# Shorter warm-up products, and the look-ups of largest weights moved forward, in a transformer layer in float32

## The chip, the cores and the metric

The kernel runs on one core of one Trainium2 chip. The metric is the device time in microseconds (us) of one execution. TensorE multiplies, VectorE (DVE in the profile), ScalarE (ACT) and GpSimd (POOL) do the elementwise work, and SyncE (SP) issues most of the transfers.

## The reference

Four sequences of 2048 tokens with 256 features go through one layer: an attention over chunks of 32 tokens with a gate, a layer norm, a gated feed-forward part whose weights are integers, and a second layer norm.

```python
Q = x @ W_q.T; K = x @ W_k.T; V = x @ W_v.T
decay = sigmoid(log_decay[0])                       # one scalar
mask = where(diff >= 0, decay ** diff, 0)           # 32 x 32
S = einsum('bncd,bnkd->bnck', Qc, Kc) * mask        # inside chunks of 32
O = einsum('bnck,bnkd->bncd', S, Vc)
attn = sigmoid(x @ W_g.T) * O @ W_o.T + x
x = layernorm(x + attn)
wg, wu, wd = w_gate / 127, w_up / 127, w_down / 127 # int32, drawn from -127 to 127
h = silu(x @ wg.T) * (x @ wu.T)                     # 768 hidden features
x = layernorm(x + h @ wd.T)
```

## The kernel before

The 8192 tokens are worked on in 16 blocks of 512 (`TB`). Everything is unrolled, and most instructions are kept in the order of the program on their engine (`in_turn`), so the order of the calls below is the order of each engine's queue. All intermediate data stay on the chip.

**Precision.** Most float32 products are made of three cheaper ones: a factor is split into a high and a low part and a "gap" term (`weight_parts`, `token_parts`), `three` multiplies high by high and low by low, lets ScalarE scale the bank (L527), and adds the product of the gaps afterwards (`rest()`, `g_rest()`, `others()`). The products have names by what they make: p_g (gate), p_v (values), p_y (scores' left factor), p_o (output projection). The first block is multiplied without splitting (pg, pv, py, pa), since its split weights aren't there yet.

**The feed-forward weights** come as nine integer pieces of 128x512: three each of `fg_int`, `fu_int` and `fd_int`, in this order numbered 0 to 8. ScalarE casts each piece to a high (fp32r) and a low (f16) copy. The split is exact only for integers up to a bound; so for each piece VectorE also looks up the largest magnitude in each row (`look_up`, L293, one TENSOR_REDUCE per piece into a column of `top`). Then `count_wide` compares `top` with the bound (`wide`, L305), adds up over the rows with a product by ones (`pw`, L309), reduces that to one number (`count`, L311) and copies it as an integer (`n_wide_early`, L1164). At the end of the program the engines read that number, and a slow path runs only if it isn't zero.

**The head.** At the start the transfers of the first weights and tokens are issued, SP taking xT and ScalarE's queue taking wg in halves. While they are under way TensorE multiplies zeros with zeros, with the column counts of `WARM` (L193, bank `pi`); these products end before pg, the gate of block 0 (L572). A float32 product is run in two passes over its columns. Then follow pv, pm (the product of two weight matrices), py, the split products of block 1, the scores and values of block 0 (ps, po), goT and pa. The sequence around the moved look-ups is:

```python
v_1, rest = split_v(1, x_parts)
cast_fg(0)
look_up([0])
sT = attn_scores(0, yT)
xTs[2] = load_xT(2)
g_rest()
rest()
look_up([1, 2])
yT, rest = split_y(1, x_parts)
goT = attn_values(0, sT, v, sg, by_half=True)
```

Some 15 us later block 0's normalized h is transposed on TensorE (`transpose_h`, bank `pt`), ScalarE makes hT_hi of it and VectorE hT_lo; `look_up([3])` stands behind that in VectorE's queue, and `gate()`, the two tanh of p_g into sg, on ScalarE. After that the output product's gap terms and the first chunk of the feed-forward part (fg, fu) follow.

**The loop** over blocks `b` interleaves block b's feed-forward chunks `hc` 0 to 5 (`ffn_up`: products fg and fu, silu on ScalarE giving s, VectorE's u = fu * s, ScalarE's u_hi, GpSimd's u_lo) with the attention of blocks b+2 and b+3. In its first pass, `look_up(range(4, 6))` stands between goT and chunk 4's u, and the last three look-ups behind chunk 5's u; in its second pass the count stands behind chunk 5.

**Banks.** The eight PSUM banks are given out from one pool in turn (`bank`). A new product's bank is one whose earlier content must have been read.

Of the kernel before, what the change touches and what calls it, by code (L numbers as in the profile page):

```python
# [47 lines left out]
F32 = mybir.dt.float32  # L48
F32R = mybir.dt.float32r
F16 = mybir.dt.float16  # L50
I32 = mybir.dt.int32
AF = mybir.ActivationFunctionType
ALU = mybir.AluOpType
# [9 lines left out]
EXACT = 128.0  # L63
# [6 lines left out]
SHIFT = 2.0**12  # L70
TOP = 1.0 - 0.5 / SHIFT
WHOLE = 1.0 + 1.0 / SHIFT
WARM = 512, 512, 128


@with_exitstack
def kernel(
# [15 lines left out]
    nc = tc.nc  # L93
# [7 lines left out]
    const = ctx.enter_context(tc.tile_pool(name="const", bufs=1))  # L101
# [12 lines left out]
    def in_turn(ins):  # L114
        tc.keep_in_program_order(ins)

    def bank(name):
        return psum.tile([P, TB], F32, tag="ps", name=name)
# [17 lines left out]
    def load_xn(b, start=None):  # L136
        xn = xin.tile([P, NG, D], F32, tag="x", name=f"x_{b}")
        src = x[span(b, start), :].rearrange("(g p) d -> p g d", p=P)
        queue(start).dma_start(xn, src)
        return xn  # L140
# [50 lines left out]
    pi = bank("pi")  # L191
    for n in WARM:
        nc.tensor.matmul(  # L193
            pi[:, :n],
            lhsT=nc.const_aps.tensor(0.0, [P, P]),
            rhs=nc.const_aps.tensor(0.0, [P, n]),
            start=True,
            stop=True,
# [88 lines left out]
    n_pieces = sum(map(len, ffn_int))  # L287
    top = const.tile([P, n_pieces], F32, tag="top", name="top")

    def look_up(which):  # L290
        pieces = [piece for pieces in ffn_int for piece in pieces]
        for i in which:
            reduced = nc.vector.tensor_reduce(  # L293
                top[:, i : i + 1],
                pieces[i].rearrange("p k n -> p (k n)"),
                mybir.AxisListType.X,
                ALU.max,
                apply_absolute_value=True,
            )
            tc.keep_in_program_order(reduced)  # L300

    def count_wide():

        wide = const.tile([P, top.shape[1]], F32, tag="wide", name="wide")
        nc.vector.tensor_scalar(wide, top, EXACT, None, ALU.is_gt)  # L305
        ones = const.tile([P, 1], F32, tag="ones", name="ones")
        nc.vector.memset(ones, 1.0)
        pw = bank("pw")
        nc.tensor.matmul(pw[:1, : top.shape[1]], lhsT=ones, rhs=wide, start=True, stop=True)  # L309
        count = const.tile([1, 1], F32, tag="count", name="count")  # L310
        nc.vector.tensor_reduce(count, pw[:1, : top.shape[1]], mybir.AxisListType.X, ALU.add)  # L311
        return count

    def free(ins):
        pass
# [101 lines left out]
    def normalize(r, scale, shift, groups=range(NG)):  # L417
        for g in groups:
            in_turn(
                nc.scalar.activation(  # L420
                    r[:, g, :],
                    r[:, g, :],
                    AF.Identity,
                    bias=shift[:, g : g + 1],
                    scale=scale[:, g : g + 1],
                )
            )
# [120 lines left out]
    def split_y(b, x_parts):  # L548
        yT = work.tile([P, KD, TB], F32, tag="yT", name=f"yT_{b}")

        def finish(i, pb):
            in_steady_turn(nc.vector.tensor_copy(yT[:, i, :], pb))

        return yT, three(f"y_{b}", feature_major(w_parts["m"], x_parts), finish)
# [479 lines left out]
    xTs[2] = load_xT(2)  # L1034
    g_rest()
    rest()
    look_up([1, 2])
    yT, rest = split_y(1, x_parts)
    goT = attn_values(0, sT, v, sg, by_half=True)
    cast_fg(1)  # L1040
# [21 lines left out]
    sg, g_rest = split_gate(2, x_parts)  # L1062
    normalize(hs[0], *scales_h)
    y_rest()
    gate = g_rest(hold=True)
    hs[1], out_rest = split_out(1, go_parts)
    hTs[0] = transpose_h(0, hs[0])
    look_up([3])
    gate()
    x_parts, x_gaps = token_parts(xTs[3], "x_3")  # L1070

# [21 lines left out]
    for b in range(NB - 2):  # L1093
        n = b + 2
        m = b + 3
        more = m < NB
        xns[n] = load_xn(n)
        if b and m + 1 < NB:
            xTs[m + 1] = load_xT(m + 1)
        hT = hTs.pop(b)  # L1100
        uT = ([], []) if b else uT_0
        sT, v, sg = ahead
        if not more:
            scales_next = iterated_scale_and_shift(mv_out, of_out, f"out_{b}")
        if b:
            normalize(hs[b + 1], *scales_h)
            up_now(b, hT, uT, 0)
        multiply = ffn_up(b, hT, uT, range(1, 2), held=True)
        if b:
            moving = move_h(b + 1, hs[b + 1])  # L1110
        else:
            cast_fd(0, range(2, 3))
            multiply()
            x_gaps()
            sT = attn_scores(n, yT)
            xTs[m + 1] = load_xT(m + 1)
        if more:
            yT, y_rest = split_y(m, x_parts)
        if b:
            multiply()  # L1120
        if not more:
            goT = attn_values(n, sT, v, sg)
        multiply = ffn_up(b, hT, uT, range(2, 3), held=True)
        if b > 1:
            normalize(r_before, *scales_out, range(NG // 2))
        multiply()
        if more:
            y_rest()
        if b == 0:
            normalize(hs[b + 1], *scales_h)  # L1130
            moving = move_h(b + 1, hs[b + 1])
        if not more:
            go_parts, go_gaps = token_parts(goT, f"go_{n}")
        multiply = ffn_up(b, hT, uT, range(3, 4), held=True)
        if b > 1:
            normalize(r_before, *scales_out, range(NG // 2, NG))
        multiply()
        if b > 1:
            store(b - 2, r_before)
        if more:  # L1140
            sT_next = attn_scores(m, yT)
            goT = attn_values(n, sT, v, sg)
            if b == 0:
                look_up(range(4, 6))
            multiply = ffn_up(b, hT, uT, range(4, 5), held=True, low_first=True)
            go_parts, go_gaps = token_parts(goT, f"go_{n}")
            if b == 0:
                cast_fd(1, range(1))
            multiply()
            go_gaps()  # L1150
            v_next, v_rest = split_v(m, x_parts)
            sg_next, g_rest = split_gate(m, x_parts)
            v_rest()
            if b == 0:
                cast_fd(1, range(1, 2))
            up_with_cast(b, hT, uT, 5, 1, range(2, 3))
            if b == 0:
                look_up(range(6, n_pieces))
            if b == 1:
                count = count_wide()  # L1160
                n_wide_early = const.tile(
                    [1, 1], I32, tag="n_wide_early", name="n_wide_early"
                )
                nc.vector.tensor_copy(n_wide_early, count)  # L1164
        else:
            up_now(b, hT, uT, 4)
            go_gaps()
        r_before = r_out
        if more:
            hs[n], out_rest = split_out(n, go_parts)  # L1170
            if b:
                hTs[b + 1] = split_h(b + 1, moving)
            g_rest()
            mv_h = out_rest()
            if b == 0:
                hTs[b + 1] = split_h(b + 1, moving)
            ahead = sT_next, v_next, sg_next
            if m + 1 < NB:
                x_parts, x_gaps = token_parts(xTs[m + 1], f"x_{m + 1}")
            std_h = root_in_turn(mv_h, of_h, f"h_{b}")  # L1180
            if b:
                mv_before, std_before = mv_out, root_in_turn(mv_out, of_out, f"out_{b}")
            back_to_silu()

            def between():
                scales = scale_and_shift(
                    mv_h, std_h, of_h, f"h_{b}", nc.vector, in_turn
                )
                if m + 1 < NB:
                    x_gaps()  # L1190
                return scales

            r_out, mv_out, scales_h = ffn_down(b, uT, hs.pop(b), between)
            if b:
                scales_out = scale_and_shift(mv_before, std_before, of_out, f"out_{b}")
        else:
            multiply = ffn_up(b, hT, uT, range(5, KH), held=True)
            hs[n], out_rest = split_out(n, go_parts)
            multiply()
            hTs[b + 1] = split_h(b + 1, moving)  # L1200
            scales_out = scales_next
            normalize(r_before, *scales_out)
            store(b - 1, r_before)

            def amid():
                return iterated_scale_and_shift(out_rest(), (HALF, 1.0), f"h_{n}")

            r_out, mv_out, scales_h = ffn_down(
                b, uT, hs.pop(b), chunkwise=True, amid=amid
            )  # L1210
            scales_out = iterated_scale_and_shift(mv_out, of_out, f"out_{b + 1}")
# [361 lines left out]
```

## Time and profile before

| | |
|---|---|
| time, median of 3 runs | 490.38 us (490.08 to 491.08) |
| the profiled execution's own time | 490.36 us |
| its span, from first to last instruction | 488.6 us |
| TensorE busy | 482.2 us (99% of the span) |
| VectorE, ScalarE, GpSimd busy | 338.1, 374.7, 281.2 us |
| look-ups (L293), each | 0.67 to 0.69 us, first at 21.3 us, last at 70.1 us |
| pw (L309) | at 97.1 us |
| warm-up products (L193) | 1.00 to 5.18 us |

In the profile PE is TensorE's products, PEld its weight loads, which overlap them; an engine's name with a q is its queue. A row of a timeline gives the start, the duration, the engine, the line, the operation, what it writes and reads, and in brackets how long the engine was idle before and what ended that. "x4" is the number of instructions in the row.

### The profile page before, as it was taken

Reading aid. Unit: us, or ns where it says so; the run is one execution under the profiler, and the core shown is the slowest. Engines: PE = TensorE matmul, PEld = TensorE weight load, DVE = VectorE, ACT = ScalarE, POOL = GpSimd, SP = SyncE. Lnnn points to the kernel's source line nnn. Section 1 sums busy time; section 2 is a strip of 40 time slices with the busy share of each in tenths; the row PEclk is TensorE's granted clock in tenths of the full one; section 3 lists DMA queues with packets and bytes.
Section 4 is the critical chain, followed back from the end, with each engine's and each line's share of the span. In section 5 each row is a group of like instructions: output and inputs, shape, how many; then the busy total and the mean of one; then the engine's idle time right before and its main releaser. Section 6 shows DMA issues by size and latency. Waiting matters only on the chain.

```text
span 488.6 us, 12295 instructions
## 1 busy us (share of the span) xinstructions
PE 482.2 (99%) x4760; PEld 382.1 (78%) x4760; DVE 338.1 (69%) x795; ACT 374.7 (77%) x699; POOL 281.2 (58%) x285
## 2 busy tenths in 40 slices
PE   9999999999999999999999999999999999999995
PEld 5788787787868878687787868878687787868674
DVE  4566988677576875757677576875757777567656
ACT  4878797687877878788787877878788787786845
POOL 2835755555745556465555745556465555657764
PEclk9999999999999999999999999999999999999999
DMA  8730411311413124131321413123131211103002
GB/s 257 234 99 19 126 49 52 79 46 36 126 30 113 44 49 128 31 101 52 100 67 33 130 33 111 45 69 105 29 103 53 79 44 37 54 20 112 34 14 84
DMA packets 43323, 36.99 MB, mean 76 GB/s; under 512 B 4864, under 2 KB 39168, under 8 KB 43264
## 3 DMA queue, kind: packets, MB, share of 16 engines
q1 hardware_dynamic: 42144, 35.28, 24.7%
q10 hardware_dynamic: 1120, 0.92, 0.6%
q8 instruction: 38, 0.62, 0.6%
q14 instruction: 21, 0.17, 0.1%
HBM read 20.45 MB, written 8.39 MB: 59 GB/s over the span
## 4 chain that ended last, share of the span: by engine, by line
PE 98%; DVE 1%; ACT 0%; issue 0%; DVEq 0%
PE fg L875 18%; PE fu L875 18%; PE fdn L730 14%; PE p_o L508 9%; PE p_y L486 9%; PE p_v L508 8%; PE p_g L486 8%; PE po L684 4%; PE ps L648 2%; PE fdn L949 2%; PE fdn L1315 1%; PE pi L193 1%; PE pg L572 1%; PE pv L614 1%; PE pa L763 1%; PE py L593 1%
## 5 line engine op out<-in xcount | busy, mean ns | idle before, releaser
L901 POOL TENSOR_TENSOR u_lo<-u,u_hi 128x512 f16<-128x512 f32 (+1 forms) x98 | 129.9, 1330 | 96.7 <-ACT u_hi L900 95.7
L895 DVE SCALAR_TENSOR_TENSOR u<-fu,s 128x512 f32<-128x512 f32 (+1 forms) x98 | 66.1, 675 | 81.2 <-ACT s L884 79.1
L884 ACT ACTIVATE s<-fg 128x512 f32<-128x512 f32 (+1 forms) x98 | 57.4, 586 | 48.1 <-PE fg L875 48.0
L900 ACT CAST u_hi<-u 128x512 fp32r<-128x512 f32 (+1 forms) x98 | 59.4, 606 | 33.1 <-DVE u L895 31.7
L875 PE MATMUL fg<-hT_hi,fg_hi 128*128 128x512 f32 (+1 forms) x196 | 72.4, 451 | 0.0
L875 PE MATMUL fu<-hT_hi,fu_hi 128*128 128x512 f32 (+1 forms) x196 | 60.5, 390 | 0.0
L875 PE MATMUL fg<-hT_lo,fg_lo 128*128 128x512 f16 (+1 forms) x196 | 58.2, 378 | 0.0
L875 PE MATMUL fu<-hT_lo,fu_lo 128*128 128x512 f16 (+1 forms) x196 | 57.4, 375 | 0.0
L467 POOL TENSOR_TENSOR go_lo<-goT,go_hi 128x512 fp32r<-128x512 f32 x30 | 44.0, 1489 | 18.5 <-ACT go_hi L466 18.5
L473 DVE SCALAR_TENSOR_TENSOR go_gap<-go_hi,goT 128x512 fp32r<-128x512 f32 x30 | 48.4, 1650 | 0.7 <-ACT go_hi L466 0.7
L467 POOL TENSOR_TENSOR x_lo<-xT,x_hi 128x512 fp32r<-128x512 f32 x30 | 37.8, 1282 | 15.2 <-ACT x_hi L466 15.2
L730 PE MATMUL fdn<-fd_hi,u_hi 128*128 128x256 f32 x312 | 44.6, 285 | 0.0
L875 PEld LDWEIGHTS fg<-hT_hi,fg_hi 128*128 128x128 f32 x196 | 35.7, 189 | 10.3
L875 PEld LDWEIGHTS fu<-hT_hi,fu_hi 128*128 128x128 f32 x196 | 36.6, 188 | 8.4
L784 DVE TENSOR_TENSOR h<-p_o,x 128x512 f32<-128x512 f32 x30 | 19.3, 685 | 31.0 <-PE p_o L508 29.1
L730 PEld LDWEIGHTS fdn<-fd_hi,u_hi 128*128 128x128 f32 x312 | 38.9, 188 | 0.3
L730 PE MATMUL fdn<-fd_lo,u_lo 128*128 128x256 f16 x312 | 38.6, 273 | 0.0
L852 POOL TENSOR_TENSOR hT_lo<-hT,hT_hi 128x512 f16<-128x512 f32 x28 | 35.4, 1289 | 3.8 <-ACT hT_hi L851 3.8
L875 PEld LDWEIGHTS <-fu_lo 128*128 128x128 f16 x196 | 19.2, 98 | 22.2
L730 PEld LDWEIGHTS <-u_lo 128*128 128x128 f16 x312 | 28.4, 98 | 3.9
L420 ACT ACTIVATE h<-h,shift_h,scale_h 128x256 f32<-128x256 f32 x52 | 27.0, 590 | 2.4 <-DVE shift_h L383 0.9
L382 POOL TENSOR_SCALAR minus_out<-rstd_out 128x4 f32<-128x4 f32 x12 | 2.7, 221 | 44.3 <-DVE rstd_out L380 44.3
(175 smaller groups left out, 1053.4 us busy)
## 6 DMA issues: line engine op xcount, KB each, us to landing
x<-in_x_dram SPq DMA_DIRECT2D x16, 512.0 KB, 3.8
xT<-in_xT_dram SPq DMA_DIRECT2D x15, 512.0 KB, 4.6
hT<-sq SPq DMA_DIRECT2D x224, 32.0 KB, 1.9
out_dram<-r SPq DMA_DIRECT2D x13, 512.0 KB, 3.3
out_dram<-r SPq DMA_DIRECT2D x7, 128.0 KB, 1.7
fg_int<-in_ffn_gT_dram SPq DMA_DIRECT2D x3, 256.0 KB, 7.9
fu_int<-in_ffn_uT_dram SPq DMA_DIRECT2D x3, 256.0 KB, 7.1
fd_int<-in_ffn_dT_dram SPq DMA_DIRECT2D x3, 256.0 KB, 5.9
```

What stands on the lines that cost most here:

```text
L420: nc.scalar.activation(r[:, g, :], r[:, g, :], AF.Identity, bias=shift[:, g : g + 1], scale=scale[:, g : g + 1],)
L467: in_turn(nc.gpsimd.tensor_tensor(lo[:, k, :], t[:, k, :], whole, ALU.subtract))
L473: nc.vector.scalar_tensor_tensor(gap[:, k, :], whole, -WHOLE, t[:, k, :], ALU.mult, ALU.add)
L486: nc.tensor.matmul(pb, lhsT=a[kind][:, k, i * P : (i + 1) * P], rhs=b[kind][:, k, :], start=kind + k == 0, stop=True, skip_group_check=True,)
L508: nc.tensor.matmul(pb[:, j * D : (j + 1) * D], lhsT=b[kind][:, k, g * P : (g + 1) * P], rhs=a[kind][:, k, :], start=kind + k + j == 0, sto ...
L730: product = nc.tensor.matmul(pb[:, j * D : (j + 1) * D], lhsT=part[:, g * P : (g + 1) * P], rhs=w, start=(i == 0), stop=(i == len(terms) - 1),
L852: nc.gpsimd.tensor_tensor(in_order[1], whole, in_order[0].bitcast(F32), ALU.subtract)
L875: product = nc.tensor.matmul(pb, lhsT=w[kind][:, dc, hc * P : (hc + 1) * P], rhs=hT[kind][:, dc, cols], start=(kind == kinds[0] and dc == ...
L884: in_turn(nc.scalar.activation(s, pg, AF.Silu, scale=SCALE / H_UP))
L895: nc.vector.scalar_tensor_tensor(u, pu, U_UP / H_UP, s, ALU.mult, ALU.mult)
L900: in_steady_turn(nc.scalar.copy(hi, u))
L901: in_steady_turn(nc.gpsimd.tensor_tensor(lo, u, hi.bitcast(F32), ALU.subtract))
```

## The change

The second of the three warm-up products gets 256 columns instead of 512. Look-ups 3, 4 and 5 join 1 and 2 behind `rest()`; look-ups 6, 7 and 8 go behind the completion of block 2's yT, followed by the comparison with the bound. The count is cut in two: `wide_counter` makes the comparison and returns a function that does the product pw, its reduction and the copy; this is called behind `transpose_h`, and its instructions are kept in order now.

```diff
-WARM = 512, 512, 128
+WARM = 512, 256, 128
...
-    def count_wide():
+    def wide_counter():
 
         wide = const.tile([P, top.shape[1]], F32, tag="wide", name="wide")
-        nc.vector.tensor_scalar(wide, top, EXACT, None, ALU.is_gt)
+        in_turn(nc.vector.tensor_scalar(wide, top, EXACT, None, ALU.is_gt))
         ones = const.tile([P, 1], F32, tag="ones", name="ones")
         nc.vector.memset(ones, 1.0)
-        pw = bank("pw")
-        nc.tensor.matmul(pw[:1, : top.shape[1]], lhsT=ones, rhs=wide, start=True, stop=True)
-        count = const.tile([1, 1], F32, tag="count", name="count")
-        nc.vector.tensor_reduce(count, pw[:1, : top.shape[1]], mybir.AxisListType.X, ALU.add)
-        return count
+
+        def count_wide():
+            pw = bank("pw")[:1, : top.shape[1]]
+            in_turn(nc.tensor.matmul(pw, lhsT=ones, rhs=wide, start=True, stop=True))
+            count = const.tile([1, 1], F32, tag="count", name="count")
+            in_turn(nc.vector.tensor_reduce(count, pw, mybir.AxisListType.X, ALU.add))
+            return count
+
+        return count_wide
...
     g_rest()
     rest()
-    look_up([1, 2])
+    look_up(range(1, 6))
     yT, rest = split_y(1, x_parts)
...
     y_rest()
+    look_up(range(6, n_pieces))
+    count_wide = wide_counter()
     gate = g_rest(hold=True)
     hs[1], out_rest = split_out(1, go_parts)
     hTs[0] = transpose_h(0, hs[0])
-    look_up([3])
+    count = count_wide()
+    n_wide_early = const.tile([1, 1], I32, tag="n_wide_early", name="n_wide_early")
+    in_turn(nc.vector.tensor_copy(n_wide_early, count))
     gate()
...
             goT = attn_values(n, sT, v, sg)
-            if b == 0:
-                look_up(range(4, 6))
             multiply = ffn_up(b, hT, uT, range(4, 5), held=True, low_first=True)
...
             up_with_cast(b, hT, uT, 5, 1, range(2, 3))
-            if b == 0:
-                look_up(range(6, n_pieces))
-            if b == 1:
-                count = count_wide()
-                n_wide_early = const.tile(
-                    [1, 1], I32, tag="n_wide_early", name="n_wide_early"
-                )
-                nc.vector.tensor_copy(n_wide_early, count)
         else:
```

## The prediction

> **What bounds the kernel now.** I read the page first (parts 1 and 4), then the timeline of the head, engine by engine, then the chain of waits around the moved steps.
>
> ```profile
> span 488.6 us, 12295 instructions
> PE 482.2 (99%) x4760; PEld 382.1 (78%) x4760; DVE 338.1 (69%) x795; ACT 374.7 (77%) x699; POOL 281.2 (58%) x285
> PE 98%; DVE 1%; ACT 0%; issue 0%; DVEq 0%
> ```
>
> TensorE is busy from 1.0 us to the last product near 483.3 us and is 98% of the chain that ended last. Work taken off VectorE is therefore worth nothing by itself; only what makes TensorE start earlier, run at another clock, or stop waiting counts. Three places are touched.
>
> First the start. These are the weight loads of the head; each is issued when the pass before it begins, so their distances are the lengths of the passes.
>
> ```profile
> 3.69 0.34 PEld L193 LDWEIGHTS pi<-const-float32-0.0 128*128 128x128 f32 x1 [0.52 <-issue]
> 4.55 0.34 PEld L193 LDWEIGHTS pi<-const-float32-0.0 128*128 128x128 f32 x1 [0.52 <-issue]
> 4.76 0.55 PEld L572 LDWEIGHTS pg<-xT,wg 128*128 128x128 f32 x2
> 5.83 0.33 PEld L572 LDWEIGHTS pg<-xT,wg 128*128 128x128 f32 x1 [0.52 <-issue]
> 6.40 0.19 PEld L572 LDWEIGHTS pg<-xT,wg 128*128 128x128 f32 x1 [0.24 <-issue]
> 6.83 0.19 PEld L572 LDWEIGHTS pg<-xT,wg 128*128 128x128 f32 x1 [0.24 <-issue]
> ```
>
> A pass of 512 columns takes 0.86 us at first (3.69 to 4.55), then 0.57 once (5.83 to 6.40), then 0.43: TensorE starts at half speed, and the full clock comes inside the 0.57 us pass, at about 6.1 us (0.27 us at half speed, 0.29 us at full). The first pass of real work, pg, runs from 4.97 to 5.83, with no wait for data.
>
> When the data came is in the landings of the first transfers (tile wg, the first issue alone, at 0.97 us):
>
> ```profile
> DMA to landing us min/median/max: 3.5/3.5/3.5
> ```
>
> So wg's first half is there at 0.97 + 3.5 = 4.47 us. The landing of xT's first half is not matched to its issue; nothing waited for it at 4.76. Its second half, by the same view, came at 1.38 + 3.9 = 5.3 us, and wg's at 1.42 + 4.1 = 5.5 us; both are wanted only after four passes.
>
> Second, VectorE around the places that look-ups leave or come to:
>
> ```profile
> 23.51 1.28 DVE L293 TENSOR_REDUCE top<-fg_int 128x1 f32<-128x512 int32 x2
> 27.23 1.41 DVE L703 SCALAR_TENSOR_TENSOR goT<-sg,po 128x256 f32<-128x256 f32 x4 [2.44 <-PE po L684]
> 41.09 1.29 DVE L552 COPY yT<-p_y 128x512 f32<-128x512 f32 x2 [0.64 <-PE p_y L486]
> 45.72 1.29 DVE L811 SCALAR_TENSOR_TENSOR hT_lo<-pt,hT_hi 128x512 f16<-128x512 f32 x2 [3.34 <-ACT hT_hi L809]
> ```
>
> The idle time in brackets (2.44 and 3.34 us) is the room. Third, the chain of waits where two look-ups stand now:
>
> ```profile
> 61.21 0.59 DVE goT L703
> 61.80 1.19 DVE top L293 x2
> 62.99 0.61 DVE u L895
> 63.60 0.02 issue
> 63.62 0.03 ACT u_hi L900
> 63.65 0.50 issue
> 64.15 0.59 ACT p_v L527
> 64.74 0.04 issue
> 64.78 1.22 PE p_v L508 x8
> ```
>
> Here alone in the region of the change the chain leaves TensorE: p_v's third product waits for ScalarE's scaling of p_v, queued behind u_hi, which waited for VectorE's u, which stood behind two look-ups. From the end of fu to the next fg TensorE takes 5.04 us here (60.96 to 66.00) and 4.66 us in the next pass of the loop (90.68 to 95.34), so the stall is 0.38 us.
>
> **The change part by part.**
>
> *Warm products.* Removed: 256 columns of the second, two passes of 0.86/2 = 0.43 us each at half speed, 0.86 us of occupancy. The warm-up would end at 4.97 - 0.86 = 4.11 us. pg cannot follow at once: wg lands at 4.47, its load then takes about 0.2 us to the first pass (4.76 to 4.97), so pg starts near 4.71 us, 0.26 us earlier, after an idle gap of 0.60 us. That gap is the added wait: all of TensorE's queue stands behind it. The 0.26 us is half-speed time, because both versions leave half speed at 6.1 us if the clock doesn't notice; worth at full speed it is 0.13 us. Bounds: 0 if xT's first half lands 0.2 us later than wg's, and 0.43 us if the data were there at 4.11. I take -0.13. Downstream this shift survives: m_sb's copy on ScalarE has 0.49 us of idle before it (wait for pm), wk lands at 2.90 + 6.2 = 9.1 us for a use at 10.5.
>
> *Does the clock notice?* The row: with TensorE busy from 1.0 us, full speed came at 6.1 us. The Trainium skill (TensorE: Matmul & The Clock Gate, Part 1: The HAM clock gate) says that a free-running window of 3413 ns is watched, and full clock follows a sustained busy window. The trace fits: the windows view gives a granted clock of 0.98 in 487.0 to 487.4 and 0.50 after, so it fell at 487.38, and 487.38 - 6.1 is 141 such windows. A window then ended at 6.1 and began at 2.7; the one before was busy for only 1.7 of 3.4 us (50%) and did not suffice. With the gap the window from 2.7 to 6.1 is busy for 2.8 us (82%). By "sustained" read strictly it fails and full speed comes at 9.5 us; by that page's later rule (HAM oscillation: no idle gaps over about 3.4 us) a gap of 0.6 us is harmless. The trace puts the threshold between 50% and 100%, no closer. By the strict reading the sum of this part is +1.57 us instead of -0.13: half of (9.52 - 4.71) less half of (6.11 - 4.97), less the 0.26. I take the harmless reading: 82% is nearer to the window that sufficed.
>
> *Look-ups 3 to 5 to 23.5 us.* Each costs 0.68 us, or 0.60 in a row (1.28 for two). Five end at 23.51 + 4 x 0.60 + 0.68 = 26.6 us; goT behind them waits for po until 27.2. The cover is 0.6 us; without it pa, and TensorE with it, would wait (it waits 0.16 us for goT as it is). ScalarE queues nothing behind it. The integers were issued on SP up to 14.8 us with 6 to 8 us to landing, so they are there by 22. Cost 0.
>
> *Look-ups 6 to 8 and the comparison to 42.3 us.* They start behind yT's copies and take 1.86 us as the three do now at 68.9, then the comparison 0.25: end 44.5. hT_lo follows at 45.7. Cost 0, cover 1.2 us. SP, POOL and the transfers are not moved past.
>
> *What they leave.* At 46.9 one look-up (0.68) makes room for the count and its copy (0.15 + 0.13); the next u waits for ScalarE's s at 48.7 anyway: 0. At 68.9 nothing gains, since h waits for p_o until 71.2. At 61.8 u follows goT directly, ending near 62.4. ScalarE then is the bound: go_hi from 61.84 to 62.9, the cast to 63.42, u_hi to 63.95 (0.53 apart), so p_v's scaling starts 0.20 us earlier than 64.15. What is late next is go_hi itself. -0.20, bounds -0.38 (the whole stall) and 0.
>
> *The count.* pw leaves 97.1 us and comes behind the transposes at 45.2. Its price there:
>
> ```profile
> 97.08 0.09 PEld L309 LDWEIGHTS pw<-wide,ones 128*1 128x1 f32 x2 [0.36 <-issue]
> 97.08 0.20 PE L309 MATMUL pw<-wide,ones 128*1 128x9 f32 x2
> ```
>
> fu's last pass starts at 96.76 and would be followed at 96.99; pw starts at 97.08, p_o at 97.21: 0.22 us, -0.22 there and +0.22 at 45.2. It waits for the comparison, done at 44.5: cover 0.7 us. On VectorE the count now sits behind hT_lo and before h's additions, in a slot shorter by 0.4 us than the look-up it replaces; at 97.3 u is no longer held by it, but TensorE did not wait there. pw also takes a PSUM bank in turn, so for the next allocations the ring of eight is one tighter: fu's first product (load at 46.40) needs the bank of p_g, whose tanh on ScalarE runs at 46.05 for 0.58. With pw ahead fu comes at 46.62: a wait of 0 to 0.1 us, I take 0. The other allocations have more room (h's additions are past by 48.5, ps needs the bank at 49.9).
>
> Sum against the profiled execution of 490.36 us (span 488.6 and 1.8 around it): -0.13 - 0.20 + 0 = -0.33, so 490.03. The median, 490.38, stands 0.02 above, so I say 490.0.
>
> **The rivals.** *The clock comes a window later* (slower). For: 18% idle in the deciding window, and "sustained". Against: 82% busy. It decides if the threshold is above 82%: +1.57 - 0.20 = +1.37, 491.7 us. *Nothing is gained*: xT's half lands last and fu waits for its bank, while ScalarE is late by itself at 64 us: 490.4. *More is gained*: data early and the stall of 0.38 gone altogether, -0.43 - 0.38: 489.6; with the window's edge also falling early, 489.1.
>
> **How the numbers follow.** 0.2% is 0.98 us, about what a measurement of this kernel can tell from no change. The clock window is free-running, and 3.4 us of phase is up to 1.7 us of end time at half rate, which fits the three times' spread of 1.0 us. Main case 0.50, own range 489.3 to 490.8; nothing gained 0.16; the late clock 0.27; more gained 0.07. Faster by over 0.98 us: most of the last case and the early tail of the main one, 0.14. Slower: nine tenths of the late clock and a little beside, 0.27. Within: 0.59. Range 489.1 to 491.9.
>
> **What would show it.** Right: pg's first load at about 4.5 us, spacing 0.43 from about 6.3, p_v's third product without a chain through look-ups, pw near 45 us, no wait of goT for anything but po. Wrong: pg passes of 0.86 us up to 9 us (the late clock); fu loads at 46 us behind ScalarE's tanh; look-ups still running when po ends.

## The result, and the profile after

| | before | after |
|---|---|---|
| median of 22 runs each, on the same chips | 490.32 us (489.29 to 491.29) | 489.25 us (488.91 to 490.37) |
| ratio, 95% interval | | 0.9981 (0.9975 to 0.9988) |
| profiled execution, its own time | 490.36 us | 489.44 us |
| its span | 488.6 us | 487.8 us |

The change is worth 0.93 us (0.59 to 1.22), 0.19%. The forecast was 490.0 us, 0.33 us less than before. The direction and the range held; the size was a third of what was measured, and most of what follows looks for the rest.

The bound hasn't moved:

```profile
span 487.8 us, 12289 instructions
PE 481.4 (99%) x4760; PEld 382.3 (78%) x4760; DVE 338.7 (69%) x795; ACT 374.5 (77%) x699; POOL 281.2 (58%) x285
PE 98%; DMA 1%; DVE 0%; ACT 0%; issue 0%
```

TensorE is 98% of the chain as before. The new 1% is "DMA": the start now waits for wg. The first line has 6 instructions less than the 12295 of before; that will matter.

**The start**, weight loads of the changed kernel:

```profile
2.84 1.19 PEld L193 LDWEIGHTS pi<-const-float32-0.0 128*128 128x128 f32 x3 [0.52 <-issue]
4.47 0.50 PEld L576 LDWEIGHTS pg<-xT,wg 128*128 128x128 f32 x2 [0.44 <-DMA wg<-in_w_gT_dram]
5.36 0.19 PEld L576 LDWEIGHTS pg<-xT,wg 128*128 128x128 f32 x1 [0.39 <-issue]
5.79 0.19 PEld L576 LDWEIGHTS pg<-xT,wg 128*128 128x128 f32 x1 [0.24 <-issue]
```

pg's first load comes at 4.47 us instead of 4.76 and waits for wg by name. The spacing is 0.43 us from 5.36 on; before it was so from 6.40 on. In this execution the full clock came at 5.22 us (the trace's clock record), not at 6.10.

**VectorE** around the moved look-ups:

```profile
22.93 1.28 DVE L293 TENSOR_REDUCE top<-fg_int 128x1 f32<-128x512 int32 x2
24.13 1.86 DVE L293 TENSOR_REDUCE top<-fu_int 128x1 f32<-128x512 int32 x3
26.62 1.41 DVE L707 SCALAR_TENSOR_TENSOR goT<-sg,po 128x256 f32<-128x256 f32 x4 [0.63 <-PE po L688]
41.69 1.86 DVE L293 TENSOR_REDUCE top<-fd_int 128x1 f32<-128x512 int32 x3
45.13 1.29 DVE L815 SCALAR_TENSOR_TENSOR hT_lo<-pt,hT_hi 128x512 f16<-128x512 f32 x2 [1.36 <-ACT hT_hi L813]
```

goT still has 0.63 us of idle time before it, ended by po, and hT_lo 1.36 us: both gaps had the room that was counted.

**Where the two look-ups stood**, the chain of the changed kernel:

```profile
60.65 1.88 PE p_v L512 x16
62.53 1.84 PE p_g L490 x8
64.37 1.11 PE p_v L512 x8
65.48 0.45 PE fg L879 x2
```

The chain no longer leaves TensorE. p_v's third product takes 1.11 us, against 0.93 in the loop's second pass (94.41 to 95.34 before), so some of the stall is left. In the waits of TensorE's loads it is a single one of 0.3 us; before, the row of the same load had 0.54 us:

```profile
PEld p_v L512 <- ACT p_v L531: 0.3, 1, 0.3
```

```profile
64.78 1.01 PEld L508 LDWEIGHTS p_v<-wv_gap,x_gap 128*128 128x128 f32 x8 [0.54 <-ACT p_v L527]
```

**The count** in its new place, and the same stretch before:

```profile
43.91 0.87 PE pt L809 x8
44.78 0.13 PE pw L311 x2
44.91 1.14 PE p_o L512 x8
46.05 0.45 PE fg L879 x2
```

```profile
44.50 0.87 PE pt L805 x8
45.38 0.94 PE p_o L508 x8
46.32 0.47 PE fg L875 x2
```

From pt to fg 2.14 us pass, against 1.82 before: pw costs 0.32 us here, of which 0.20 appears as a longer p_o behind it.

### The profile page after: what moved, and what is told of

Same layout as the page of the kernel before. It is cut to its first block, busy times and chain, and to the rows that moved or that the text cites. A ratio compares the mean times of both kernels' runs of the same rounds, so it can differ in the third digit from the quotient of the medians.

```text
span 487.8 us, 12289 instructions
## 1 busy us (share of the span) xinstructions
PE 481.4 (99%) x4760; PEld 382.3 (78%) x4760; DVE 338.7 (69%) x795; ACT 374.5 (77%) x699; POOL 281.2 (58%) x285
## 4 chain that ended last, share of the span: by engine, by line
PE 98%; DMA 1%; DVE 0%; ACT 0%; issue 0%
PE fg L879 18%; PE fu L879 18%; PE fdn L734 14%; PE p_v L512 9%; PE p_o L512 9%; PE p_y L490 9%; PE p_g L490 9%; PE po L688 4%; PE ps L652 2%; PE fdn L953 2%; PE fdn L1313 1%; PE pg L576 1%; DMA wg<-in_w_gT_dram 1%; PE pa L767 1%; PE pv L618 1%; PE py L597 1%
## 5 line engine op out<-in xcount | busy, mean ns | idle before, releaser
L879 PEld LDWEIGHTS <-fg_lo 128*128 128x128 f16 x196 | 13.1, 98 | 19.2 <-issue 12.8
```

Of the source, the lines that this page charges most:

```text
L879: product = nc.tensor.matmul(pb, lhsT=w[kind][:, dc, hc * P : (hc + 1) * P], rhs=hT[kind][:, dc, cols], start=(kind == kinds[0] and dc == ...
```

## The experiments

Three theories stood at first. A: the gain is the sum that was forecast, and the rest is where the clock's free-running window fell. B: the shorter warm-up itself brings the full clock forward. C: the moved look-ups and the count are worth more than the one stall. D and E came later, for the time outside the span. The table is the key to all experiments. Each row is one profiled execution, in us. "Full clock" is the time at which the trace's clock record goes to full speed; "pv" and "pt to end" are the start of the first pv, and the time from the first transpose to the end of the span, on the chain; "around" is the execution's own time less its span. The ratio alone is not of that one execution: it is over all timed runs of the kernel to those of before on the same chips.

| kernel | full clock | pv | pt to end | around | ratio (95%) |
|---|---|---|---|---|---|
| before | 6.10 | 9.14 | 444.12 | 1.74 | |
| two_lookups | 6.38 | 9.28 | 443.87 | 2.22 | 1.0002 (0.9993 to 1.0010) |
| warm_only | 4.58 | 8.26 | 444.23 | 2.02 | 1.0001 (0.9992 to 1.0010) |
| rest_only | 5.70 | 8.93 | 443.85 | 1.55 | 0.9989 (0.9981 to 0.9997) |
| changed | 5.22 | 8.53 | 443.90 | 1.63 | 0.9981 (0.9975 to 0.9988) |
| changed, again | 6.73 | 9.17 | 443.98 | 1.63 | 0.9987 (0.9980 to 0.9993) |
| fill | 6.14 | 8.94 | 443.87 | 1.62 | 0.9985 (0.9978 to 0.9991) |
| cast_early | 4.86 | 8.30 | 443.75 | 1.63 | 0.9978 (0.9971 to 0.9985) |
| shorter | 8.36 | 10.12 | 443.86 | 1.56 | 1.0025 (1.0015 to 1.0034) |
| none | 10.48 | 11.12 | 443.83 | 1.55 | 1.0022 (1.0015 to 1.0030) |
| pad_dve | 6.83 | 9.31 | 443.85 | 1.65 | 0.9984 (0.9977 to 0.9991) |
| pad_act | 5.52 | 8.69 | 443.87 | 1.76 | 0.9986 (0.9977 to 0.9995) |
| pad_pool | 5.54 | 8.74 | 443.89 | 2.08 | 0.9990 (0.9982 to 0.9999) |
| pad_all | 4.05 | 8.19 | 443.87 | 1.63 | 0.9993 (0.9985 to 1.0002) |

From pv to pt every kernel takes 35.32 to 35.42 us. So a span is three things: when pv starts, that constant, and the stretch from pt to the end. The first hangs on the clock; the last is the same to 0.15 us in all kernels that share the look-ups' places.

### One part at a time

**warm_only**: before, with the shorter warm-up alone.

```diff
-WARM = 512, 512, 128
+WARM = 512, 256, 128
```

> The kernel before with only the second warm-up product cut to 256 columns; look-ups and count stay where they were. Theory A (the cut saves only the 0.3 us until the data come, at half speed, and the edge of the clock's window falls by chance): 0.13 to 0.17 us faster than before, and the full clock may come anywhere between about 4.4 and 8 us. Theory B (the shorter warm-up itself lets the full clock come sooner): 0.6 to 0.9 us faster, and the full clock comes before 5.5 us again. Theory C (the look-ups and the count are worth more than the one stall): 0 to 0.2 us faster.

Measured: 490.10 us, ratio 1.0001 (0.9992 to 1.0010), so between 0.4 us faster and 0.5 slower: theory A's 0.15 lies inside, theory B's 0.6 to 0.9 does not. The clock did come at 4.58 us, but later profiles with the same warm-up have it at 6.73 and 6.83. Theory B is out.

**rest_only**: the changed kernel with `WARM = 512, 512, 128`.

> The changed kernel with the old warm-up products (512, 512, 128): look-ups and count moved, nothing else. Theory A and theory B: 0.25 us faster than before, the part of the stall at p_v's third product that goes; pw costs the same at both places. Theory C: 0.7 us or more faster.

Measured: 489.72 us, ratio 0.9989, 0.54 us faster (0.15 to 0.93). In the profile pt to end is 0.27 us shorter than before. The timing leaves theory A's 0.25 possible, but sits higher; why, the time outside the span will show.

**two_lookups**: before, with look-ups 4 and 5 alone moved.

```diff
-    look_up([1, 2])
+    look_up([1, 2, 4, 5])
...
-            if b == 0:
-                look_up(range(4, 6))
```

> The kernel before with only look-ups 4 and 5 taken from between goT and u to the early place; everything else as before. Theories A and B: this alone holds the gain of the look-ups, 0.2 to 0.25 us faster than before, with p_v's third product still waiting 0.3 us for ScalarE. Theory C: clearly less than the changed kernel with the old warm-up gains.

Measured: pt to end 443.87 us, 0.25 us less than before and equal to the whole of rest_only: in the profile these two look-ups hold the entire gain, and the other four moves with the count nothing. Yet the timed runs say 1.0002 (0.9993 to 1.0010), an interval that just holds the 0.9995 of those 0.25 us. And the profiled execution took 2.22 us around its span, where rest_only's took 1.55. That was the first sign of something outside the span.

### How the clock answers to the warm-up

**shorter**: the changed kernel with `WARM = 512, 128`.

> The changed kernel with the second warm-up product left out (512, 128): the warm-up ends near 3.3 us, and TensorE is idle for about 1.2 us before pg. Theory A with a threshold under 60% busy: the same as the changed kernel within 0.1 us, since pg is bound by the data. Theory A with a threshold of 80% or so: the clock's window with the gap is lost, 1 to 1.7 us slower than the changed kernel, slower than before. Theory B: faster still than the changed kernel, or the same.

```profile
4.53 0.50 PEld L576 LDWEIGHTS pg<-xT,wg 128*128 128x128 f32 x2 [1.35 <-DMA wg<-in_w_gT_dram]
5.54 0.34 PEld L576 LDWEIGHTS pg<-xT,wg 128*128 128x128 f32 x1 [0.52 <-issue]
8.11 0.32 PEld L576 LDWEIGHTS pg<-xT,wg 128*128 128x128 f32 x1 [0.52 <-issue]
8.66 0.19 PEld L576 LDWEIGHTS pg<-xT,wg 128*128 128x128 f32 x1 [0.24 <-issue]
```

pg's load comes 0.06 us later than in the changed kernel, after 1.35 us of idle, but the passes stay at 0.86 us until 8.1, and full clock comes at 8.36. Slower than before by 1.2 us (0.7 to 1.7). This is the rival that the prediction feared, one product further on.

**none**: the changed kernel with `WARM = ()`.

> The changed kernel without any warm-up product: TensorE first works at 4.5 us. Theory A: the clock's window can only be busy from then on, so full clock comes between 7.5 and 11.3 us, mean near 9.4, where it came at 5.2 in the changed kernel; pg starts at 4.7 all the same. Slower than the changed kernel by half of the difference, 1.1 to 3 us, some 1.5 to 2 us slower than before. Were the full clock tied to something other than TensorE's activity, it would come at 5 to 6 us and nothing would be lost.

```profile
4.42 6.70 PE L576 MATMUL pg<-xT,wg 128*128 128x512 f32 x8 [4.42 <-DMA wg<-in_w_gT_dram]
```

pg takes 6.70 us instead of 4.06; full clock at 10.48 us. Slower than before by 1.1 us, less than the 1.5 to 2 expected; its spans alone are 1.53 us longer on average (1.29 to 1.76), which is what was expected, and the rest lies outside the span (below).

**after_again** and **fill** (`WARM = 512, 384, 128`: the warm-up ends as the data come).

> The changed kernel once more. The profiles so far obey one sum: from pt to the end the moved look-ups give 0.26 us, the shorter warm-up gives 0.17 us at an equal time of full clock, and the rest is half of the difference in when the full clock comes. Theory A (the two gains of 0.4 us are all; what was measured beyond them was where the clock's window fell in those runs): a ratio of 0.9991 to 0.9992, 0.4 us faster. Theory B (the change brings the full clock forward by itself): 0.998 again, 0.9 to 1.1 us faster.

> The changed kernel with the second warm-up product of 384 columns: the warm-up then ends at about 4.5 us, just when the data come, so there is no idle gap. Theory A: pg starts within 0.1 us of the changed kernel's, 0.35 to 0.4 us faster than before, and no execution loses a clock window. Theory B (the gap or the shorter products bring the clock forward): 0.3 to 0.6 us slower than the changed kernel.

Measured: 489.64 us, 0.64 faster than before (0.34 to 0.98) for the changed kernel, and 489.70, 0.74 faster (0.44 to 1.08) for fill. The first lies between the theories' numbers, and its interval holds 0.4 as well as 0.9. In fill pg's passes follow the warm-up without a gap, and it is as fast as the changed kernel, so no help or harm of the gap is seen. Whether theory A's two gains are all, these ratios don't decide.

### What is left of the stall

**cast_early**: fill, with one more move, ScalarE's first cast of fd_lo.

```diff
+            if b == 0:
+                cast_fd(1, range(1))
             go_parts, go_gaps = token_parts(goT, f"go_{n}")
-            if b == 0:
-                cast_fd(1, range(1))
             multiply()
```

> The same with 384 columns, and one more move: ScalarE's first cast of fd_lo ahead of go_hi, into the 0.67 us in which ScalarE waits for goT. If the rest of the stall at p_v's third product is ScalarE's queue, it goes: 0.12 to 0.18 us off the stretch from pt to the end, beside the 0.26 us; no wait for p_v's scaling is left. If go_hi or x_gap is what is late, the wait stays and nothing changes.

```profile
60.55 0.61 ACT L282 CAST fd_lo<-fd_int 128x512 f16<-128x512 int32 x1
61.33 1.16 ACT L470 ACTIVATE go_hi<-goT 128x512 fp32r<-128x512 f32 x2 [0.16 <-DVE goT L707]
62.39 0.61 ACT L904 CAST u_hi<-u 128x512 fp32r<-128x512 f32 x1
62.90 1.06 ACT L531 ACTIVATE p_v<-p_v 128x512 f32<-128x512 f32 x2
```

The cast fills the time in which ScalarE waits for goT, u_hi follows go_hi directly, and the wait for p_v's scaling is gone from the list of waits. pt to end falls by a further 0.12 us (443.75 against fill's 443.87). At 489.42 us, 1.1 us faster than before (0.74 to 1.42), it has the lowest ratio measured here, though its interval overlaps the changed kernel's.

### Outside the span

Sorted by "around", the kernels made from the one before had 1.74, 2.02 and 2.22 us, those made from the changed one, up to cast_early, 1.55 to 1.63. The view of the transfers after the span shows the first group apart. Before, then the changed kernel, each in the 3 us from 488.7 us:

```profile
DMA packets 1, 0.01 MB, mean 3 GB/s; under 512 B 0, under 2 KB 0, under 8 KB 0
q14 instruction: 1, 0.01, 0.9%
```

```profile
DMA packets 0, 0.00 MB, mean 0 GB/s; under 512 B 0, under 2 KB 0, under 8 KB 0
```

Queue q14 carries instructions. In before, one packet of 8192 bytes is moved 1.8 us after the last recorded instruction (two in warm_only and two_lookups, 1.8 to 2.2 us after it), and none in the changed kernel. Of the six recorded instructions that went, all semaphore waits, two are ScalarE's, two TensorE's, one VectorE's and one GpSimd's. Four kernels put such a number back on VectorE, ScalarE or GpSimd with idle work at the head:

```diff
     in_turn(nc.scalar.activation(table, eps, AF.Sigmoid))
+    in_turn(nc.scalar.activation(table, eps, AF.Sigmoid))
+    in_turn(nc.scalar.activation(table, eps, AF.Sigmoid))
...
     nc.vector.memset(half, -0.5)
+    nc.vector.memset(half, -0.5)
...
         nc.gpsimd.memset(sT, 0.0)
+    nc.gpsimd.memset(sTs[1], 0.0)
```

The first pair is pad_act, the second addition pad_dve, the third pad_pool; pad_all has all of them.

> What is to be settled: kernels made from the one before take 1.74 to 2.22 us around their span (profiled execution's own time less span), those made from the changed one 1.55 to 1.63, and only the first show an instruction transfer (queue q14) about 2 us after the last recorded instruction. The changed kernel has 2 recorded instructions less on ScalarE, 1 on VectorE and 1 on GpSimd. Here they are put back as idle ones in the head, where the engines have room: two more sigmoids of one column on ScalarE, one memset of 128x4 on VectorE, one memset of sT on GpSimd. Theory D (the end of the program lay just past the last block of instructions that had been fetched): the late transfer is back, the time around the span is 1.7 us or more, and the kernel is 0.2 to 0.5 us slower than the changed one without any change from pt to the last product. Theory E (the late transfer came with the place of the count, or by chance): no late transfer, 1.55 to 1.65 us around the span, a ratio to before of about 0.9985.

> Two more one-column sigmoids on ScalarE in the head, nothing else added to the changed kernel. Theory D, if the block is ScalarE's: the late transfer of q14 is back, with 1.7 us or more around the span. Otherwise as the changed kernel, 1.55 to 1.65.

> One more memset on VectorE in the head, nothing else added to the changed kernel. Theory D, if the block is VectorE's: the late transfer of q14 is back, with 1.7 us or more around the span. Otherwise 1.55 to 1.65.

> One more memset of sT on GpSimd in the head, nothing else added to the changed kernel. Theory D, if the block is GpSimd's: the late transfer of q14 is back, with 1.7 us or more around the span. Otherwise 1.55 to 1.65.

The late transfer is back in pad_act, pad_pool and pad_all, and absent in pad_dve. In the same 3 us, pad_act and then pad_pool:

```profile
q14 instruction: 1, 0.01, 0.7%
```

```profile
q14 instruction: 1, 0.01, 0.8%
```

In the span nothing differs (pt to end 443.85 to 443.89). What it costs is read from all timed runs, since the span of each is on record too (to 0.1 us). The time around it:

| kernel | timed runs | around, median (lowest to highest) |
|---|---|---|
| before | 166 | 2.09 (1.61 to 2.32) |
| warm_only | 14 | 2.04 (1.69 to 2.25) |
| two_lookups | 13 | 2.17 (1.79 to 2.25) |
| changed, again, rest_only, fill, cast_early, shorter, none | 131 | 1.58 (1.50 to 1.67) |
| pad_dve | 21 | 1.59 (1.53 to 1.67) |
| pad_act | 13 | 1.77 (1.69 to 1.86) |
| pad_pool | 13 | six 1.63 to 1.69, seven 2.10 to 2.24 |
| pad_all | 14 | 2.09 (1.67 to 2.28) |

The kernels without the late transfer stand apart. Against before on the same chips, the changed kernel measured again has 0.46 us less around its span on average (0.41 to 0.51; intervals are 95%, by resampling the runs), where warm_only and two_lookups have nothing less. ScalarE's two instructions bring 0.17 us back (0.13 to 0.20, against pad_dve), GpSimd's one 0.33 (0.19 to 0.48), some 0.5 us in half of the runs and next to nothing in the others, and both together the whole, 0.46 (0.35 to 0.55). Theory D is borne out as to the engines, the sign and the size. The medians of the whole times show it less well (pad_dve 489.77 us, pad_act 489.66, pad_pool 490.10, pad_all 490.17), since the phase of the clock scatters the spans by more than this, 1.4 us for full clocks from 4.05 to 6.83.

That ScalarE's program and GpSimd's each ended just past a block of instructions before, and within it after, fits all this, but the ends of the blocks are not in the profile. How the transfer costs time is open too. If the measured time begins with the span, the transfer starts within 0.2 us of its end, so whether the engines wait for it, or it is only the mark of a longer way to the end, wasn't shown. In before's trace all engines run the branches at the slow path near 486 us. The Trainium skill (Runtime: NRT & Kernel Launch, Instruction fetch mechanics) says that a taken branch to a place outside the fetched blocks forces a fetch before work can go on; the late transfer comes over 3 us after these branches, the trace doesn't say whether one was taken, and no run here shows such a wait.

## Why the prediction was right or wrong

**The bound**: right. Nothing that VectorE was relieved of counted but the one stall.

**Warm products, -0.13 us**: right in mechanism. The old warm-up's three profiles lie on pv = 9.14 + (T - 6.10)/2, T being the time of full clock: 9.28 at 6.38, 8.93 at 5.70. Where T comes well after pg's load, the new warm-up is earlier than this line by 0.17 us (T 5.22), 0.28 (6.73), 0.20 (6.83), 0.16 (5.52) and 0.12 (5.54), 0.19 on average. It varies because wg doesn't always land alike: pg's load went at 4.27 us in the one with 0.28, at 4.59 in the last. The other two profiles of this warm-up, against the line carried on below 5.70, have 0.12 (T 4.58 in warm_only, load at 4.56) and 0.07 us later instead of earlier (T 4.05 in pad_all, so that the gap fell in time at full speed). All seven average 0.14. By the timed runs alone this part can't be told from 0 (warm_only). The loads were idle for 0.44 us and not 0.60, since the 0.60 ran to pg's first pass and so held the load as well.

**The clock**: the harmless reading was right in every profile of this warm-up. T ranges from 4.05 to 6.83 us in the seven of them (5.70 to 6.38 in the three with the old warm-up). In every trace the clock falls again 481.28 us later, or 477.87 in shorter and none; the two differ by one window of 3.41 us and are 141 and 140 of them. If the share of a window in which TensorE is busy decides, the runs narrow the threshold. The windows that ended one window ahead of full clock did not suffice: at 3.42 us in pad_dve (busy from 1.00 us, 71%), at 4.95 in shorter (some 63%) and at 7.07 in none (busy from pg's load at 4.42, 78%). The one that ended at 4.58 in warm_only with the gap in it did (86%). So the threshold lies between some 78% and 86%; the prediction had 50% to 100%. The 82% that it reckoned with were never tried: in the first profile of the changed kernel the deciding window ended at 5.22, and the gap in it, from the forecast end of the warm-up at 4.11 to the load at 4.47, leaves some 89%. That the gap was harmless is thus in part owed to its being shorter than forecast.

The late clock may still be there at times: among 119 timed runs of this warm-up one of warm_only (492.25 us) and one of pad_all (491.86) have spans of 490.0 and 490.1 us, over 1 us longer than every other of their kernel, as a lost window would make them; of the 166 of before one span is 490.1. No trace of these was kept.

In the pair of profiles first compared, 0.44 us of the 0.61 by which pv is earlier was only this phase, half of 6.10 less 5.22.

**Look-ups 4 and 5, -0.20 us**: right, slightly small. 0.25 us by two_lookups. What is late next is ScalarE's queue, as said, but not go_hi: cast_early left go_hi at its place behind goT, took the cast out from behind it, and the wait went, for 0.12 us more. **All other moves at 0**: right, by rest_only being equal to two_lookups from pt to end.

**The count, +0.22 and -0.22**: the balance was right, the price too small. It is 0.32 us at either place: the loop's second pass, between its and the first's down product, went from 29.66 to 29.34 us. What was missed is that p_o behind so small a product takes longer, by the 0.20 us of the rows above; why it does isn't shown. The tighter ring of banks cost nothing that shows: fu's load goes at 46.11 us, without a wait.

**The sum** failed in a term that it held constant: "span 488.6 and 1.8 around it". The 1.8 us were carried over unchanged, without a reason, but fewer instructions on ScalarE and GpSimd moved the ends of their programs, and the time around the span went down by 0.46 us (0.41 to 0.51). Within the span the forecast was good: over the changed kernel measured again and its four pads, which do the same work there, the spans are 0.32 us shorter than before (0.18 to 0.45), for a forecast of 0.33. The two make 0.78, inside the intervals of 0.93 (0.59 to 1.22) and of 0.64 (0.34 to 0.98). So the direction was earned in the span, but more than half of the gain came from a term that the prediction put at nothing; that this term also went down, and not up, is luck as far as the prediction goes.

## What to carry to other kernels

When one engine is busy for 99% of the time, cut the trace at two or three of its instructions and compare the stretches: here the stretches repeat within 0.15 us, where whole runs of the changed kernel spread over 1.5 us (488.91 to 490.37), as a full clock that comes anywhere between 4.05 and 6.83 us makes them. Compare also each execution's own time with its span, over all timed runs; a difference there is not in any engine's row. A warm-up ahead of the first data could end a little early here (0.44 us of idle loads), but not by 1.35 us.

## What was not expected of the hardware

- The number of instructions can cost time although no instruction does: two idle sigmoids of one column on ScalarE, or one memset on GpSimd, bring a late transfer on the queue of instructions back, with 0.17 and 0.33 us, and all pads together 0.46 us.
- 1.35 us of idle TensorE in the warm-up (shorter) cost 1.2 us against before, as much as no warm-up at all (none, 1.1 us); in the spans alone 1.5 us each.
- pw, two passes of 9 columns, takes 0.13 us by its own rows and 0.32 us of TensorE's time.
